# A state-space layer's hand-written round order: cross products to the top, once-a-group work to the middle, exponentials last

## The chip, the cores and the metric

The kernel runs on one core of one Trainium2 chip. A core has engines that each work through their own list of instructions in order: TensorE (PE, matrix products), VectorE (DVE), ScalarE (ACT), GpSimd (POOL) and SyncE (SP, which here only issues DMAs). They wait for each other through semaphores. The metric is device time of one execution in microseconds (us). Three timed runs of the kernel before gave 2692.72, 2696.85 and 2704.56 us, a median of 2696.85.

## The reference, cut to what matters

A decoder of four blocks with twelve layers works on x, 32 sequences of 128 tokens of 128 features. Only the first layer, a state-space layer, is touched:

```
x = x + attn0(layernorm(x))          # then eleven more layers
# attn0, for every sequence, in two chunks of 64 tokens:
z, xBC, dt = split(u @ in_proj.T)            # 256, 512, 32 columns
xBC = silu(causal depthwise conv, 4 taps)    # 256 of x, 128 of B, 128 of C
dt  = 0.001 + 0.099 * sigmoid(dt + dt_bias);  dA = -exp(A_log) * dt
Acum = cumsum(dA in the chunk)
Yd = sum_s (C.B)[q,s] * exp(Acum[q] - Acum[s]) * x[s] * dt[s]       # s <= q, 32 heads of 8
Yo = C . (state of the chunk before) * exp(Acum)                     # chunk 2 only
y  = (Yd + Yo + D*x) * silu(z);  y = y * rsqrt(mean(y^2)) * norm_w
x  = x + layernorm(u) + layernorm(y @ out_proj.T)                    # u: the normalized x
```

## The kernel before, in words

`layer0` treats the 32 sequences in eight groups (`i`) of four (`j`). There is one round per sequence, n = 4i + j, and two rounds of run-up (n = -2 and -1). The order on PE, DVE and ACT is written out by hand: `follow(T, A, V)` makes every instruction of such an engine come after the one recorded before it, so program order is queue order. POOL keeps its written order only in the prologue. All operations are recorded in one helper, so the profile gives nearly all of them line 194; they are told apart by their tiles.

What a round does, with the names used below:

- `first(n+2)`: PE forms decays and C.B for the sequence two rounds on; ACT copies them into a tile `cbl` and takes one exponential; POOL forms `right`. Then PE transposes the convolved x, ACT copies it (the "xt copy", 128x256) and POOL makes two scaled copies `xd`, `xe` and masks `cbl`.
- `second(n+1)`: four matmuls into two `two` tiles (the exponents). `exponentials(n+1)`: two ACT exponentials of 128x1024. `weighted(n+1, h)`: two DVE products of 128x1024 (`bbig<-bbig,cbl`), here called w0 and w1.
- `third(n)`: 64 small products into `acc`, and then the **cross part**: four matmuls (the state of the first chunk, and the decay), an ACT copy into `cbl` (the "cross copy") and a DVE product of 128x128 (`gmid<-cbl`, the "cross product").
- `conv(g, c)`: one of four channel blocks per round, in five steps: matmul and ACT copy; ACT scale; three DVE updates (`gmid<-bmid,w,gmid`); ACT tanh; a last DVE product (`gmid<-bmid,gmid`). Block 2, which falls in the rounds with j = 1, is done by four matmuls over 512 columns instead (`ps<-xnT,taps`, "the taps", 8 instructions in the trace), an ACT activation, a tanh and the last DVE product.

Once a group: `entry(g)` (layer norm of x: statistics; a scale; four ACT activations "xn"; four transposes and their copy; four more ACT activations "x acts" and a POOL addition), `decays(g)` (dt: matmuls; a DVE addition `dts<-ps,ww`; tanh; six DVE steps; a matmul and an exponential; a product), `gate(g, b)` twice (matmul, ACT copy, ACT tanh; a DVE product into `z`) and `joined(g)` in six steps S1 to S6 (S1: D*x plus the sums; S2: times silu(z); S3: two ACT squares and a POOL addition; S4: the output product of 16 instructions and its copy; S5: the mean-square matmul, statistics, `s<-ps`; S6: scale and addition into x).

PE results go through one-bank PSUM tiles `ps`, of which there are two, used in turn: the result after next can't be written before ACT or DVE has read the one two back. `bmid` has five buffers and `gmid` ten, taken in the same way.

Of the kernel before, what the change touches and what calls it, by code (L numbers as in the profile page):

```python
# [23 lines left out]
G = 8  # L24
J = 4
# [180 lines left out]
def program(ctx, tc, cols, x, ctxt, mask, drop, dfirst, dsmall, dwide, drows, dunits, dexperts, dconst, drel, dwq, out):  # L206
    nc = tc.nc
    V, A, T = (Ordered(tc, engine) for engine in (nc.vector, nc.scalar, nc.tensor))
    P, SY = Ordered(tc, nc.gpsimd), nc.sync
# [10 lines left out]
    def ps(shape=(128, 512), dtype=F32):  # L220
        return pp.tile(list(shape), dtype, tag="ps", name="ps", bufs=2)
# [14 lines left out]
    def gmid(shape=(128, 512), dtype=F32):  # L236
        return mid.tile(list(shape), dtype, tag="gmid", name="gmid", bufs=10)
# [42 lines left out]
    ident = K["ident"]  # L280
# [3 lines left out]
    for i in range(G):  # L284
        t = const.tile([128, J, D], F32, name=f"x{i}")
        SY.dma_start(out=t, in_=x[i * J : i * J + J].rearrange("b s d -> s b d"))
        xg.append(t)
        if i == 0:
            SY.dma_start(out=ident, in_=dconst[:, 0:128])
            SY.dma_start(out=cs[:, 128:], in_=dconst[:, 128 : cconst.kept])  # L290
            w0 = units.tile([128, cfirst.n], F32, tag="unit", name="w0")
            A.dma_start(out=w0, in_=dfirst)
            ww = const.tile([128, cwide.n], F32, name="ww")
            A.dma_start(out=ww[:, 0 : cwide.early], in_=dwide[:, 0 : cwide.early].to_broadcast([128, cwide.early]))
    taps = units.tile([128, UNIT], F32, tag="unit", name="taps")
    SY.dma_start(out=ww[:, cwide.early :], in_=dwide[:, cwide.early :].to_broadcast([128, cwide.n - cwide.early]))
    wr = const.tile([1, crows.n], F32, name="wr")
# [17 lines left out]
    onesb = const.tile([128, 128], BF16, name="onesb")  # L315
    V.memset(onesb, 1.0)
    identb = const.tile([128, 128], BF16, name="identb")
    V.tensor_copy(identb, ident)

    pick16 = const.tile([128, 4], BF16, name="pick16")  # L320
    V.tensor_copy(pick16, K["pick16"])
    flip = const.tile([128, 128], BF16, name="flip")
    V.tensor_copy(flip, W0["flip"])
    ctxT = [const.tile([128, 512], F32, name=f"ctxT{i}") for i in range(G)]


# [489 lines left out]
    def layer0(lead):  # L816
# [3 lines left out]
        def weights():  # L820

            A.activation(na, WW["m_A_log"], AF.Exp)
            V.tensor_scalar(na, na, -1.0, None, ALU.mult)
            yield
            for b in range(2):
                mean, block = small(1), W0["out"][:, b * 128 : b * 128 + 128]
                V.tensor_scalar(block, block, W0["norm_w"][:, b : b + 1], None, ALU.mult)
                V.tensor_reduce(mean, block, AX.X, ALU.add)
                V.tensor_scalar(mean, mean, -1.0 / 128, None, ALU.mult)
                V.tensor_scalar(block, block, mean[:, 0:1], None, ALU.add)  # L830
            V.tensor_scalar(W0["D"], W0["D"], 0.25, None, ALU.mult)
            yield

        block2 = W0["xbc"][:, 256:384]
# [2 lines left out]
        def make_taps():  # L837

            d, p = bmid((128, 4, 128)), ps((128, 4, 128))
            V.tensor_tensor(d, bc(ident, 1, 4), bc(W0["cw"][:, 8:12], 2, 128), ALU.mult)  # L840
            mm(flat(p), block2, flat(d))
            A.copy(taps[:, 0:512], flat(p))

        kept = [gbig((128, 2, 1024)) for _ in range(3)]
        more = bbig()
        sides = [kept[0][:, n].rearrange("p (j s r c) -> p j s r c", j=J, s=2, r=4) for n in range(2)]

        def fill():
            for t in (*kept[0:2], more):
                P.memset(t, 0.0)  # L850
            for t in sides:
                for token, side, at in ((0, 0, 0), (64, 0, 8), (0, 1, 16)):
                    one = bc(bc(ident[:, token : token + 1], 1, J), 2, 4)
                    P.tensor_copy(t[:, :, side, :, at : at + 8], one.to_broadcast([128, J, 4, 8]))

        xds = [t.rearrange("p (a n m e) -> p a n m e", a=8, n=4, m=4) for t in (kept[1][:, 0], kept[1][:, 1], more[:, 0:1024])]
        rights = [kept[2][:, n, 0:512].rearrange("p (a k) -> p a k", a=8) for n in range(2)]
# [159 lines left out]
        def third(n):  # L1017

            i, j = n // J, n % J
            (xd, xe, cbl, _), m = fronts.pop(n), mids.pop(n)[0].rearrange("p s h q -> p (s h) q")  # L1020
            if j == 0:
                sums[i] = [acc((128, 2, J, 64)) for _ in range(2)]
                offs[i] = gmid((128, 2, J, 64))
            for b in range(2):
                for k in range(4):
                    for r in range(4):
                        for ch in range(2):
                            rows = slice(64 * ch, 64 * ch + 64)
                            mm(sums[i][ch][32 * r : 32 * r + 32, b, j], flat(xd[rows, 4 * b + r, k]), m[rows, 16 * b + 4 * r + k],
                               k == 0, k == 3)  # L1030
            p = ps((128, 2, 2, 64))
            for b in range(2):
                mm(p[:, 0, b], xe[:, 128 * b : 128 * b + 128], cbl[0:64, 64:128])
            for b in range(2):
                mm(p[:, 1, b], K["spread"][:, 128 * b : 128 * b + 128], cbl[:, 320:384])
            A.copy(cbl[:, 128:384], p.rearrange("p s b q -> p (s b q)"))
            both = cbl[:, 128:384].rearrange("p (s b q) -> p s b q", s=2, b=2)
            V.tensor_tensor(offs[i][:, :, j], both[:, 0], both[:, 1], ALU.mult)
# [50 lines left out]
        def go(what, g, *more):  # L1089

            if 0 <= g < G:
                key = what, g, *more
                if key not in late:
                    late[key] = what(g, *more)
                next(late[key], None)
# [6 lines left out]
        go(entry, 0)  # L1102
        go(entry, 0)
        fill()
        make_taps()
        go(entry, 0)
        next(prepared)
        go(conv, 0, 2)
        go(decays, 0)
        go(conv, 0, 3)  # L1110
        go(conv, 0, 2)
        go(entry, 1)
        go(conv, 0, 3)
        go(decays, 0)
        go(conv, 0, 2)
        go(conv, 0, 3)
        go(conv, 0, 0)
        go(decays, 0)
        go(entry, 1)
        go(conv, 0, 3)  # L1120
        go(conv, 0, 0)
        go(conv, 0, 1)
        go(decays, 0)
        go(conv, 0, 3)
        go(entry, 1)
        go(conv, 0, 0)
        go(conv, 0, 1)
        go(conv, 0, 0)
        go(conv, 0, 1)
        go(entry, 1)  # L1130
        go(conv, 0, 0)
        go(decays, 0)
        go(conv, 0, 1)
        go(conv, 0, 1)
        next(prepared)
# [2 lines left out]
        for n in range(-2, G * J):  # L1138
            i, j = n // J, n % J

            convs_now = [(1, 2)] if n == -2 else [(1, 3), (1, 0)] if n == -1 else [(i + 1, 1) if j == 0 else (i + 2, (2, 3, 0)[j - 1])]

            def go_conv():
                for g, c in convs_now:
                    go(conv, g, c)

            front = first(n + 2) if n + 2 < G * J else iter(())
            next(front, None)
            go_conv()
            next(front, None)  # L1150
            go_conv()
            if j == 0:
                go(decays, i + 1)
                go(gate, i, 0)
                go(joined, i - 2)
            elif j == 1:
                go(joined, i - 1)
            elif j == 2:
                go(decays, i + 2)
                go(decays, i + 2)  # L1160
                go(entry, i + 3)
                go(joined, i - 1)
            elif j == 3:
                go(gate, i + 1, 1)
                go(entry, i + 3)
                go(joined, i - 1)
            if 0 <= n + 1 < G * J:
                second(n + 1)
            go_conv()
            if 0 <= n + 1 < G * J:  # L1170
                exponentials(n + 1)
            if j == 1:
                go(joined, i - 1)
            elif j == 3:
                go(entry, i + 3)
            if 0 <= n + 1 < G * J:
                weighted(n + 1, 0)
            if 0 <= n < G * J:
                third(n)
            if 0 <= n + 1 < G * J:  # L1180
                weighted(n + 1, 1)
            if j == 0:
                go(entry, i + 2)
                go_conv()
            elif j == 1:
                go(entry, i + 2)
            elif j == 2:
                go(decays, i + 2)
                go(gate, i + 1, 1)
                go_conv()  # L1190
            elif j == 3:
                go(joined, i)
                go(gate, i + 1, 0)
                go_conv()
                go(decays, i + 2)
            go_conv()
            if n == -1:
                go(entry, 1)
            if n >= G * J - 5:
                next(lead)  # L1200
        next(lead)
        go(joined, G - 1)
# [1311 lines left out]
```

## Time and profile before

| | us |
|---|---|
| median of three timed runs (range) | 2696.85 (2692.72 to 2704.56) |
| the profiled execution's own time | 2692.69 |
| its span in the trace | 2690.9 |
| the first layer in it, roughly | 0 to 327 |
| busy in 90 to 270 us (180 us): PE, DVE, ACT, POOL | 166.6, 160.8, 122.4, 94.5 |

A timeline line reads: start in us, time taken, engine, line, operation, tile written <- tiles read, shape, number of merged instructions, and in brackets the engine's idle time before it with what ended it. `PE` is the matmul, `PEld` the load of its weights. A line of the windows view gives the stretch, its length, the busy time of each engine asked for with the count of instructions, then the TensorE clock that was granted (1.00 is full), the DMA share and GB/s.

### The profile page before, as it was taken

The page shows a single profiled execution, that of the slowest core. Times are in us where ns is not written, and L with a number is a line of the kernel's source. Part 1 is how long each engine was busy: PE and PEld are TensorE (multiplying, and loading weights), DVE is VectorE, ACT ScalarE, POOL GpSimd, SP SyncE. Part 2 cuts the span into 40 slices and gives each one's busy share as a digit, 9 for nine tenths or more (in the row PEclk, how much of TensorE's full clock was granted, in tenths as well). Part 3 has the DMA queues.
Part 4 walks back from the last instruction along what each step waited for, and adds up shares of the span by engine and source line. Part 5 has one row for each costly group of instructions (what it writes and reads, how often), then busy time and mean ns, then how long its engine had stood idle before and what let it go on. Part 6 is the DMA issues. An engine that isn't in the chain of part 4 may idle for free.

```text
span 2690.9 us, 59184 instructions
## 1 busy us (share of the span) xinstructions
PE 2387.5 (89%) x24663; PEld 1527.2 (57%) x24663; DVE 1983.8 (74%) x3972; ACT 1347.3 (50%) x2999; POOL 927.1 (34%) x979
## 2 busy tenths in 40 slices
PE   6999889999989999999998999988888987887755
PEld 3665567777744435556764444446665886544434
DVE  6888778888888756777776555569996338898993
ACT  5766544444422223344443445468983334665653
POOL 3454532322310214345651101144443444332432
PEclk8999899999999999999998999999998998998886
DMA  3000000000000010000000000000003463100000
GB/s 113 3 2 14 10 21 5 9 5 4 18 12 1 0 36 3 3 14 14 12 3 17 1 0 1 1 1 2 2 2 129 147 214 130 62 16 16 28 12 20
DMA packets 51966, 74.23 MB, mean 28 GB/s; under 512 B 4017, under 2 KB 42450, under 8 KB 51570
## 3 DMA queue, kind: packets, MB, share of 16 engines
q1 hardware_dynamic: 48786, 64.10, 7.5%
q0 software_dynamic: 2624, 5.40, 0.6%
q8 instruction: 194, 3.18, 0.5%
q10 hardware_dynamic: 288, 0.95, 0.1%
q14 instruction: 74, 0.61, 0.1%
HBM read 57.54 MB, written 12.89 MB: 26 GB/s over the span
## 4 chain that ended last, share of the span: by engine, by line
PE 56%; DVE 22%; ACT 6%; issue 2%; POOL 2%; DMA 0%; DVEq 0%; ACTq 0%; POOLq 0%
PE two L194 20%; PE ps L194 18%; PE acc L194 17%; DVE bbig L194 9%; DVE s L194 7%; ACT bbig L194 3%; DVE bmid L194 3%; POOL xn L194 1%; DVE x L194 1%; ACT bmid L194 1%; DVE gmid L194 1%; POOL s L194 1%; DVE h L194 0%; ACT L194 0%; ACT gmid L194 0%
## 5 line engine op out<-in xcount | busy, mean ns | idle before, releaser
L194 PE MATMUL two<-xnT,u 128*128 128x512 f32 x512 | 261.7, 612 | 9.3 <-ACT bmid L194 5.6
L194 DVE TENSOR_REDUCE s<-two 128x8 f32<-128x1024 f32 (+1 forms) x192 | 228.8, 1219 | 47.6 <-PE two L194 43.0
L194 DVE TENSOR_TENSOR bbig<-bbig 128x1024 f32<-128x1024 f32 (+3 forms) x232 | 248.2, 1111 | 14.3 <-ACT bbig L194 12.0
L194 PE MATMUL acc<-bmid,u 128*128 128x512 f32 x416 | 215.0, 603 | 13.4 <-DVE bmid L194 12.4
L194 PE MATMUL ps<-cs,bbig 128*128 128x128 f32 x1184 | 176.5, 289 | 47.6 <-ACT bbig L194 21.3
L194 DVE TENSOR_TENSOR bmid<-bmid,ps 128x512 f32<-128x512 f32 x192 | 129.9, 684 | 93.1 <-ACT bmid L194 71.0
L194 PEld LDWEIGHTS ps<-cs,bbig 128*128 128x128 f32 x1184 | 135.1, 146 | 101.2 <-ACT bbig L194 36.5
L194 PE MATMUL two<-gbig,gmid 32*128 32x512 f32 (+1 forms) x1248 | 186.3, 551 | 4.4 <-issue 2.1
L194 POOL TENSOR_TENSOR s<-s,nhalf 128x4 f32<-128x4 f32 x104 | 128.7, 1237 | 135.1 <-DVE s L194 116.5
L194 PEld LDWEIGHTS two<-xnT,u 128*128 128x128 f32 x512 | 91.4, 191 | 115.7 <-issue 56.6
L194 ACT ACTIVATE bbig<-two 128x1024 f32<-128x1024 f32 x96 | 94.8, 1025 | 116.7 <-PE acc L194 101.7
L194 DVE RECIPROCAL s<-acc 128x128 f32<-128x128 f32 x96 | 91.3, 951 | 83.6 <-PE acc L194 83.4
L194 ACT COPY bbig<-ps 128x512 f32<-128x512 f32 x166 | 91.4, 585 | 116.4 <-PE ps L194 116.3
L194 POOL TENSOR_TENSOR x<-x,ww 128x512 f32<-128x512 f32 x64 | 91.6, 1431 | 163.1 <-ACT xn L194 80.3
L194 ACT ACTIVATE bmid<-two,ws 128x512 f32<-128x512 f32 x128 | 85.2, 686 | 111.6 <-PE two L194 111.4
L194 POOL TENSOR_TENSOR bbig<-bbig,s 128x1024 f32<-128x1024 f32 x32 | 61.7, 1927 | 222.6 <-PE two L194 152.5
L194 ACT ACTIVATE bmid<-two 128x512 f32<-128x512 f32 x88 | 52.5, 597 | 164.0 <-PE two L194 159.2
L194 PEld LDWEIGHTS acc<-bmid,u 128*128 128x128 f32 x416 | 75.0, 192 | 101.0 <-issue 46.1
L194 ACT ACTIVATE bbig<-two,s 128x256 f32<-128x256 f32 x256 | 118.1, 477 | 25.4 <-DVE s L194 25.3
L194 ACT ACTIVATE bbig<-bbig,s 128x128 f32<-128x128 f32 x384 | 118.8, 390 | 6.8 <-DVE s L194 6.8
L194 POOL TENSOR_SCALAR gbig<-bmid,cs 128x512 f32<-128x512 f32 x64 | 99.2, 1566 | 49.0 <-ACT bmid L194 49.0
L194 PE MATMUL two<-xT,we 128*128 128x128 f32 (+1 forms) x576 | 100.4, 330 | 15.9 <-ACT xT L194 9.8
(331 smaller groups left out, 6267.0 us busy)
## 6 DMA issues: line engine op xcount, KB each, us to landing
we<-in_experts SPq DMA_DIRECT2D x36, 768.0 KB, 4.6
u<-in_units SPq DMA_DIRECT2D x10, 768.0 KB, 4.3
gmid<-in_ctx SPq DMA_DIRECT2D x16, 256.0 KB, 3.0
x<-in_x SPq DMA_DIRECT2D x8, 256.0 KB, 5.6
gmid<-in_mask SPq DMA_DIRECT2D x8, 256.0 KB, 3.1
ys<-bbig SPq DMA_DIRECT2D x2, 1024.0 KB, 6.2
gmid<-ys SPq DMA_DIRECT2D x8, 256.0 KB, 3.1
gmid<-in_drop SPq DMA_DIRECT2D x8, 256.0 KB, 3.5
```

Source lines behind the costliest of these rows:

```text
L194: d = self.made = f(*args, **kwargs)
```

## The change

The cross part becomes a function of its own, `cross(n)`, called at the very top of round n, ahead of `first(n+2)`; `third(n)` keeps the 64 small products. The once-a-group steps that stood between the exponentials and w0, and many of those that stood after w1, go to the middle of a round, ahead of `second(n+1)`; what is left after w1 is the end of the convolution and few steps. S3 and S4 now stand together in the round with j = 2. The prologue is put in another order (block 3's convolution and the first `decays` ahead of the taps), the first two DMAs on ACT's queue change places, three small DVE casts move from the program's start into the weights' preparation, one of `fill`'s three memsets is taken first, and the next layer's first preparatory step is taken one round earlier.

```diff
-            A.dma_start(out=w0, in_=dfirst)
             ww = const.tile([128, cwide.n], F32, name="ww")
             A.dma_start(out=ww[:, 0 : cwide.early], in_=dwide[:, 0 : cwide.early].to_broadcast([128, cwide.early]))
+            A.dma_start(out=w0, in_=dfirst)
...
-    V.tensor_copy(identb, ident)
...
-    V.tensor_copy(pick16, K["pick16"])
...
-    V.tensor_copy(flip, W0["flip"])
...
             V.tensor_scalar(W0["D"], W0["D"], 0.25, None, ALU.mult)
+            V.tensor_copy(identb, ident)
+            V.tensor_copy(pick16, K["pick16"])
+            V.tensor_copy(flip, W0["flip"])
             yield
...
+        def cross(n):
+            i, j = n // J, n % J
+            _, xe, cbl, _ = fronts[n]
+            if j == 0:
+                offs[i] = gmid((128, 2, J, 64))
             p = ps((128, 2, 2, 64))
             for b in range(2):
                 mm(p[:, 0, b], xe[:, 128 * b : 128 * b + 128], cbl[0:64, 64:128])
...
-        go(entry, 0)
+        go(conv, 0, 3)
+        go(decays, 0)
+        go(conv, 0, 3)
+        go(conv, 0, 2)
...
+            if 0 <= n:
+                cross(n)
             front = first(n + 2) if n + 2 < G * J else iter(())
...
                 go(joined, i - 2)
+                go(entry, i + 2)
             elif j == 1:
                 go(joined, i - 1)
+                go(entry, i + 2)
             elif j == 2:
                 go(decays, i + 2)
+                go(joined, i - 1)
+                go(joined, i - 1)
                 go(decays, i + 2)
+                go(gate, i + 1, 1)
                 go(entry, i + 3)
-                go(joined, i - 1)
             elif j == 3:
                 go(gate, i + 1, 1)
+                go(gate, i + 1, 0)
+                go(decays, i + 2)
                 go(entry, i + 3)
                 go(joined, i - 1)
             if 0 <= n + 1 < G * J:
...
                 exponentials(n + 1)
-            if j == 1:
-                go(joined, i - 1)
-            elif j == 3:
-                go(entry, i + 3)
-            if 0 <= n + 1 < G * J:
                 weighted(n + 1, 0)
...
             if j == 0:
-                go(entry, i + 2)
                 go_conv()
-            elif j == 1:
-                go(entry, i + 2)
             elif j == 2:
                 go(decays, i + 2)
-                go(gate, i + 1, 1)
+                go(entry, i + 3)
                 go_conv()
             elif j == 3:
                 go(joined, i)
-                go(gate, i + 1, 0)
                 go_conv()
-                go(decays, i + 2)
             go_conv()
...
-            if n >= G * J - 5:
+            if n >= G * J - 6 and n != G * J - 5:
                 next(lead)
```

More of the change, by code (lines that the diff above doesn't have):

```diff
@@ L848, in fill @@
         def fill():
-            for t in (*kept[0:2], more):
-                P.memset(t, 0.0)
+            P.memset(kept[0], 0.0)
             for t in sides:
@@ L854, in fill @@
                     P.tensor_copy(t[:, :, side, :, at : at + 8], one.to_broadcast([128, J, 4, 8]))
+            for t in (kept[1], more):
+                P.memset(t, 0.0)
         xds = [t.rearrange("p (a n m e) -> p a n m e", a=8, n=4, m=4) for t in (kept[1][:, 0], kept[1][:, 1], more[:, 0:1024])]
@@ L1019, in third @@
             i, j = n // J, n % J
-            (xd, xe, cbl, _), m = fronts.pop(n), mids.pop(n)[0].rearrange("p s h q -> p (s h) q")
+            xd, m = fronts.pop(n)[0], mids.pop(n)[0].rearrange("p s h q -> p (s h) q")
             if j == 0:
                 sums[i] = [acc((128, 2, J, 64)) for _ in range(2)]
-                offs[i] = gmid((128, 2, J, 64))
             for b in range(2):
@@ L1104, in layer0 @@
         fill()
+        go(entry, 0)
         make_taps()
-        go(entry, 0)
+        go(conv, 0, 3)
+        go(decays, 0)
+        go(conv, 0, 3)
+        go(conv, 0, 2)
+        go(decays, 0)
+        go(entry, 1)
+        go(conv, 0, 3)
         next(prepared)
+        go(decays, 0)
+        go(conv, 0, 0)
         go(conv, 0, 2)
@@ L1110, in layer0 @@
         go(conv, 0, 3)
+        go(conv, 0, 0)
         go(conv, 0, 2)
@@ L1113, in layer0 @@
         go(conv, 0, 3)
-        go(decays, 0)
-        go(conv, 0, 2)
-        go(conv, 0, 3)
+        go(conv, 0, 1)
+        go(conv, 0, 0)
+        go(entry, 1)
+        go(conv, 0, 1)
         go(conv, 0, 0)
@@ L1119, in layer0 @@
         go(entry, 1)
[L1120 to L1126, printed above, removed]
         go(conv, 0, 1)
         go(conv, 0, 0)
[L1129 to L1132, printed above, removed]
         go(conv, 0, 1)
```

## The prediction

> **What bounds the kernel now.** The change touches only the first layer, so I read the stretch it takes. First the windows view over 90 to 270 us, a steady part of that layer (VectorE's busy time stands third, behind the two columns of PE):
>
> ```profile
> 90.00:270.00 180.00, 166.60 (x3172) 109.74 (x3174) 160.77 (x305) 122.35 (x248) 94.50 (x94) 0.94 0.02 7
> ```
>
> PE (166.6 of 180) and DVE (160.8) are both nearly full, so neither alone sets the pace: what matters is where one waits for the other. The waits view of that stretch, DVE only:
>
> ```profile
> DVE gmid L194 <- ACT bmid L194: 6.2, 3, 2.6
> DVE dts L194 <- PE ps L194: 6.2, 5, 1.3
> DVE gmid L194 <- ACT cbl L194: 3.8, 7, 0.9
> DVE bbig L194 <- ACT bbig L194: 0.9, 3, 0.3
> ```
>
> 17 us of waits: for the tanh of block 2 (6.2), for the matmuls of `decays` (6.2), for the cross copy (3.8; this one the change attacks), for exponentials (0.9). Then the timeline of the group where they are shortest, from the end of DVE's three updates with j = 0 (call it X, 136.6) to the addition `dts` with j = 2 (call it Y, 148.0):
>
> ```profile
> 136.03 3.66 PE L194 MATMUL ps<-xnT,taps 128*128 128x512 f32 x8
> 136.55 1.21 DVE L194 SCALAR_TENSOR_TENSOR bbig<-bbig,cbl 128x1024 f32<-128x1024 f32 x1
> 139.73 0.69 ACT L194 ACTIVATE gmid<-ps,w 128x512 f32<-128x512 f32 x1 [1.94 <-PE ps L194]
> 140.57 0.64 ACT L194 ACTIVATE bmid<-gmid 128x512 f32<-128x512 f32 x1
> 141.10 1.94 ACT L194 ACTIVATE bbig<-two 128x1024 f32<-128x1024 f32 x2
> 142.91 1.17 ACT L194 ACTIVATE bmid<-z 128x512 f32<-128x512 f32 x2
> 143.95 0.39 ACT L194 COPY cbl<-ps 128x256 f32<-128x256 f32 x1
> 144.20 1.67 ACT L194 ACTIVATE x<-x,s 128x128 f32<-128x128 f32 x4
> 146.17 0.61 ACT L194 COPY bmid<-ps 128x512 f32<-128x512 f32 x1
> 146.84 1.08 PE L194 MATMUL ps<-w,xnT 128*128 128x32 f32 x8
> 148.03 0.29 DVE L194 TENSOR_TENSOR dts<-ps,ww 128x128 f32<-128x128 f32 x1 [1.12 <-PE ps L194]
> ```
>
> The chain to Y runs taps, block 2's activation and tanh, exponentials, squares (1.17), cross copy, x acts (1.67), copies, `decays`. The exponentials end at 143.0, before DVE takes w0 at 143.3: hidden. Starts of neighbours lie closer than the durations say (w0 to next 1.14, two exponentials 1.81, x acts 1.55); I use these spacings. X to Y is 11.4, 11.5, 14.7, 13.1 and 14.7 us in the groups from 98.8, 136.6, 173.2, 213.5 and 251.7, and 16.1 in the first (60.9 to 77.0): mean 13.6. Y to the next X is 26.3, 25.2, 25.5, 25.2 and 24.9 (21.8 in the first group, without `joined`). The long X to Y have a reason on PE:
>
> ```profile
> 171.65 1.22 PE L194 MATMUL ps<-w,gbig 128*128 128x64 f32 x4 [1.03 <-ACT cbl L194]
> 173.53 6.10 PE L194 MATMUL ps<-xnT,taps 128*128 128x512 f32 x8
> ...
> 172.00:179.00 7.00, 7.00 (x17) 0.54 0.00 0
> ```
>
> Here the granted clock was 0.54 (last line, windows view, PE only) and the taps took 6.10 us, not 3.66.
>
> **The change, step by step.** All instructions stay; only places move.
>
> 1. *X to Y.* Before, block 2's taps stood behind a `ps` bank that the cross copy and the xnT copy freed ahead of the tanh of block 1, so they began 0.5 us before X. Now ACT does that tanh first (it waits for X: 0.1 + 0.55), then the cross copy (0.4), whose bank the taps take: they start at X + 1.1, end at X + 4.75. Activation and xt copy to 5.6, tanh to 6.25. Then the x acts, now ahead of the exponentials: 7.75; first exponential 8.7, second 9.6; cross copy 9.95. DVE is through w0, w1, block 1's last product, cross product and S2 at X + 4.3 (2.28 + 0.6 + 0.2 + 1.2), waits 2.0 for the tanh, does 0.6, waits 1.8 for the exponential, does w0, w1, cross product (to 11.2). PE's next conv matmul (1.1) needs the cross copy's bank: 11.05; its copy 11.6; `decays` 1.0: Y = X + 12.75. That is 1.3 over the undisturbed 11.45, though the squares (1.05) have left the chain.
>
> 2. *The clock.* In rounds with j = 0 the four transposes of `entry` now stand behind the conv copy, and that waits on ACT for DVE's last product of the round before (before, ACT waited 2.49 us there, but PE had other work). Laid out, PE is through at Y + 17.9 and gets the copy at 21.2: idle 3.3 us, then 5.2 us of work before the taps. In the trace, 1.0 to 1.2 us of idleness at that place was followed by the half clock in three groups of the last four with taps, and not in 134.96. If half clock follows, 6.8 us long as at 172, the 5.2 us become about 8.6, a start of the taps 2.2 later: X + 14.95. With as many such groups as before (4 of 6): (2 x 12.75 + 4 x 14.95) / 6 = 14.2; with all, 14.95. Against 13.6: +0.6 to +1.35, six times: +3.7 to +8.1; without any, 12.75: -5. I take +5.5. The Trainium skill ("TensorE: Matmul & The Clock Gate", "What's actually happening") says the clock falls to half after an idle window of about 3.4 us and comes back after a busy one; the row at 172 agrees in length (two such windows), not in the idleness needed (1.0). By that rule a 3.3 us idle stretch is at the edge in every group: 6 x 1.35 = 8.1, speaking against the change.
>
> 3. *Y to X, j = 2.* `gate`'s matmul (1.1), copy and tanh (1.1) now precede the exponentials: first exponential at Y + 4.95, DVE free at 3.7 to 4.1: +0.85. *j = 3:* the mean-square matmul now queues behind a second `gate`, through two `ps` banks: conv copy Y + 8.95, gate matmul 10.1, its copy 10.75, mean-square 11.85; DVE is there at 10.1 to 10.95 and waits 1.0 to 1.8: 1.4. Ends for both together: nothing, if ACT and PE run further ahead than laid out, and 2.65. The rest of the stretch is DVE alone: 22.9 before, plus one cross product (0.2).
>
> 4. *POOL's part in DVE's time.* Before, 25.2 - 22.9 = 2.3 us of Y to X is lengthening, as in `z<-bmid,z` at 1.53 (157.16, beside a POOL operation) against 0.68 at 167.97. Where a wait follows, it is swallowed. Kept: nothing to 2.2; I take 0.8 to 1.1, as only the stretch after step 3's wait has none behind it. Y to X = 23.1 + 2.25 + 0.95 = 26.3 to 26.8 against 25.2 to 25.5: +1.2 to +1.5, five times, and +0.5 in the first group: +7.5.
>
> 5. *Cross product.* The 3.8 us of waits for its copy are inside the stretches above; now the copy is long done.
>
> 6. *Prologue.* The casts (0.23, 0.17, 0.22) leave the first norm, but its next DVE instructions read constants landing at 9.81, so xn still starts near 10.6. Transposes ahead of the taps' making bring xnT from 15.84 to 13.3; statistics (1.5) and three updates (2.2) fall into DVE's 6.9 us wait before 23.15; but `decays` stays behind block 2's activation on ACT (24). Laying the rest end to end, the second `dts` (42.02) comes at 39.5: -2.5 (ends: 0, if the taps stay cold longer; -5). The weights' DMA, issued 0.43 later, had landed by 9.16 and is needed at 10.6: nothing; if not, up to +0.5. `fill`'s order: nothing, as the first fold waits for DVE.
>
> 7. *End.* In the last rounds the cross product waited 0.63 to 0.71; its chain is gone: -1 (0 to -2). The next layer's step a round earlier: 0 +- 1.
>
> Sum: 5.5 + 7.5 - 2.5 - 1 = +9.5 on the profiled execution's own 2692.69 (span 2690.9): 2702.2. That execution was the fastest of those shown, 4.2 below the median 2696.85; in terms of that median 2706.
>
> **Rivals.**
> - *Slower by more.* PE's idle stretch brings half clock in every group and reaches into the taps: 6.10 for 3.66, so Y = X + 12.75 + 2.4 + 0.9 (other matmuls): +2.5 x 6 = 15; and DVE's lengthening stays at 2.2: +2.5 x 5 = 12.5. With -2.5: +25, 2722. For it: PE's share of 0.93; against: taps start after most of the half-clock stretch. It decides when PE's stop lasts over a second longer than the 1.0 to 1.2 that sufficed.
> - *Faster.* PE keeps its full clock: with conv and cross at the top, the 1.0 to 1.2 us stop right ahead of the taps is gone, and nothing halves the clock: X to Y 12.75 for 13.6, -0.85 x 6 = -5; Y to X at 24.4 (waits of step 3 hidden, half the lengthening), -0.8 x 5 = -4; -3.5 for prologue and end: -12.5, between -8 and -22 (the lower end if none of the 17 us of waits comes back): 2684. For it: two groups (98.8, 136.6) show it can stay full; against: step 2's idle stretch. It decides where no window of PEclk in a j = 0 to 1 stretch falls under 0.9.
>
> **Numbers.** My case 0.50 (+3 to +17; a fifth of it beyond +13.5), slower by more 0.28, faster 0.22. A measurement of this kernel tells about 0.5%, 13.5 us, from no change. Slower: 0.28 + 0.10 = 0.38. Faster: a little over half of the faster case lies beyond -13.5 us if it is as wide as its bounds: 0.12. Same: 0.50. My case alone: 2700 to 2714; to hold eight in ten the range takes in most of both rivals: 2682 to 2724.
>
> **What would show it.** DVE waits of 1.5 to 2 us in every group for block 2's tanh (`gmid<-bmid` from ACT) and then for w0 (`bbig` from ACT); about 1 us for `s<-ps` from PE; no waits for `gmid<-cbl`; PEclk near 0.5 around each j = 0 to 1 turn; the second `dts` near 39.5; Y to Y near 40 us for 37.8 to 39.9. I am wrong if w0 with j = 1 starts less than 7 us after X, or if the layer's last DVE product falls before 327.

## The result and the profile after

| | before | after |
|---|---|---|
| median of eight runs each on one chip, us (range) | 2694.78 (2686.91 to 2704.56) | 2707.28 (2701.53 to 2711.34) |
| ratio after / before | | 1.0044, 95% interval 1.0022 to 1.0065 |
| span of the profiled execution, us | 2690.9 | 2705.3 |

The changed kernel is slower by 0.44%, 12.5 us; +9.5 us was predicted, put as 2706 against the earlier median of 2696.85. The traces show the stop on PE that the prediction named, but also that three terms of the sum were mis-sized. Their errors cancelled, so how close the total came is luck.

The windows view of the changed kernel over 90 to 270 us (columns as for before):

```profile
90.00:270.00 180.00, 156.76 (x2865) 103.76 (x2866) 146.75 (x291) 111.57 (x221) 78.81 (x84) 0.87 0.01 2
```

Every engine does less in the same 180 us, DVE 146.8 us for 160.8, and the granted clock is 0.87 for 0.94. The waits view says for what DVE waits (90 to 275 us):

```profile
DVE gmid L194 <- ACT bmid L194: 22.0, 4, 7.1
DVE bbig L194 <- ACT bbig L194: 7.2, 4, 1.8
DVE dts L194 <- PE ps L194: 2.0, 4, 0.5
```

and for what PE waits:

```profile
PE ps L194 <- ACT bmid L194: 18.2, 13, 3.5
PE ps L194 <- ACT cbl L194: 3.1, 5, 1.7
```

DVE no longer waits for the cross copy. It waits 7 us for block 2's tanh in three of these four groups (1.0 in the other), and PE stops for 3.3 to 3.5 us ahead of `entry`'s transposes in four of groups 2 to 6. The timeline of one turn from j = 0 to j = 1 shows how the two hang together:

```profile
172.18 0.38 PE L194 MATMUL ps<-cs,gmid 128*128 128x128 f32 x2
175.44 0.58 ACT L194 COPY bmid<-ps 128x512 f32<-128x512 f32 x1 [3.67 <-DVE gmid L194]
176.08 1.12 PE L194 MATMUL ps<-cs,xn 128*128 128x128 f32 x4 [3.51 <-ACT bmid L194]
180.94 2.35 DVE L194 SCALAR_TENSOR_TENSOR bbig<-bbig,cbl 128x1024 f32<-128x1024 f32 x2
181.12 0.63 ACT L194 ACTIVATE bmid<-gmid 128x512 f32<-128x512 f32 x1
183.38 0.37 ACT L194 COPY cbl<-ps 128x256 f32<-128x256 f32 x1 [1.63 <-PE ps L194]
184.91 5.45 PE L194 MATMUL ps<-xnT,taps 128*128 128x512 f32 x7
192.32 0.69 DVE L194 SCALAR_TENSOR_TENSOR gmid<-bmid,gmid 128x512 f32<-128x512 f32 x1 [7.02 <-ACT bmid L194]
194.83 2.56 DVE L194 SCALAR_TENSOR_TENSOR bbig<-bbig,cbl 128x1024 f32<-128x1024 f32 x2 [1.81 <-ACT bbig L194]
198.94 0.29 DVE L194 TENSOR_TENSOR dts<-ps,ww 128x128 f32<-128x128 f32 x1 [0.51 <-PE ps L194]
```

ACT's conv copy waits 3.67 us for a `bmid` buffer that DVE's last product of the round before frees; PE's transposes of `entry` wait for the bank behind that copy; then X (180.94), and Y comes 18.0 us later. The windows view, PE only, of the same turn (length, busy, granted clock):

```profile
172.00:176.00 4.00, 0.56 (x3) 0.97 0.01 4
176.00:189.00 13.00, 12.92 (x163) 0.50 0.01 1
190.00:200.00 10.00, 9.18 (x182) 1.00 0.01 2
```

After the stop PE runs 13 us at half clock, which takes in the taps (5.45 us for seven of their eight instructions in the line above, 5.87 for all eight).

Where the 14.4 us between the two spans come from, read off at X and Y of each group in both traces, and at one marker behind the first layer, the next layer's first product `bbig<-bbig,s` (367.29 us before, 379.28 after):

| stretch | before | after | difference |
|---|---|---|---|
| start to the first X | 60.9 | 57.5 | -3.4 |
| X to Y, six groups | 16.1, 11.4, 11.5, 14.7, 13.1, 14.7 | 18.6, 12.95, 17.9, 18.0, 18.0, 18.1 | +22.0 |
| Y to X, six times | 21.8, 26.3, 25.2, 25.5, 25.2, 24.9 | 21.5, 26.3, 26.3, 26.3, 26.3, 26.3 | +4.0 |
| last X to the marker | 75.9 | 65.4 | -10.5 |
| marker to the end | 2323.6 | 2326.0 | +2.4 |

The last row is the same program in both; in the traces shown in this document it takes between 2320 and 2333 us, and eight runs of before alone spread over 18 us, so it is taken as scatter here.

### The profile page after: what moved, and what is told of

Read it like the earlier page. It is cut to its first block, busy times and chain, and to the rows that moved or that the text cites. A ratio compares the mean times of both kernels' runs of the same rounds, so it can differ in the third digit from the quotient of the medians.

```text
span 2705.3 us, 59213 instructions
## 1 busy us (share of the span) xinstructions
PE 2391.3 (88%) x24644; PEld 1532.2 (57%) x24663; DVE 1983.4 (73%) x3972; ACT 1347.6 (50%) x2999; POOL 920.2 (34%) x979
## 4 chain that ended last, share of the span: by engine, by line
PE 62%; DVE 24%; ACT 8%; issue 3%; POOL 2%; DMA 1%; SPq 0%; DVEq 0%; ACTq 0%; POOLq 0%
PE ps L194 24%; PE two L194 21%; PE acc L194 18%; DVE bbig L194 9%; DVE s L194 7%; ACT bbig L194 4%; DVE bmid L194 3%; DVE gmid L194 2%; ACT bmid L194 1%; POOL xn L194 1%; DVE x L194 1%; POOL s L194 1%; DMA we<-in_experts 1%; ACT gmid L194 0%; ACT xn L194 0%
## 5 line engine op out<-in xcount | busy, mean ns | idle before, releaser
L194 DVE TENSOR_REDUCE s<-two 128x8 f32<-128x1024 f32 (+1 forms) x192 | 228.8, 1219 | 48.9 <-PE two L194 44.2
L194 PE MATMUL ps<-cs,bbig 128*128 128x128 f32 x1184 | 177.5, 290 | 46.5 <-ACT bbig L194 21.1
L194 PEld LDWEIGHTS two<-xnT,u 128*128 128x128 f32 x512 | 91.4, 191 | 115.6 <-issue 56.6
L194 PE MATMUL two<-xT,we 128*128 128x128 f32 (+1 forms) x576 | 102.2, 334 | 13.7 <-ACT xT L194 9.8
```

The lines of the kernel that those rows point to most:

```text
L194: d = self.made = f(*args, **kwargs)
```

## The experiments

Theory: PE's 3.5 us stop at `entry`'s transposes brings the half clock, and that makes X to Y long. Rivals: the chain alone does it (the taps' bank behind block 1's tanh, x acts ahead of the exponentials), whatever the clock; or half clock comes anyway from shorter stops. In the table, "layer" is the time of the marker above in the run's trace less 367.29, from one execution each (it can lie at the edge of the run's range, as in e3).

| run | median, us | ratio to before (95%) | X to Y, groups 2 to 6 | layer |
|---|---|---|---|---|
| before | 2694.8 | | 11.4, 11.5, 14.7, 13.1, 14.7 | 0 |
| after | 2707.3 | 1.0044 (1.0022 to 1.0065) | 12.95, 17.9, 18.0, 18.0, 18.1 | +12.0 |
| e1 entry back | 2695.1 | 1.0003 (0.9990 to 1.0016) | 12.9, 14.8, 14.7, 14.9, 14.6 | -1.5 |
| e2 warm | 2694.1 | 1.0004 (0.9989 to 1.0020) | 13.1, 12.95, 14.7, 14.9, 14.6 | -4.8 |
| e3 entry alone | 2703.3 | 1.0036 (1.0019 to 1.0053) | 11.7, 13.5, 13.3, 16.9, 14.0 | +0.9 |
| e4 lead back | 2713.8 | 1.0072 (1.0051 to 1.0094) | 12.95, 17.9, 18.0, 18.05, 18.1 | +15.6 |
| e5 entry back, late tanh | 2686.4 | 0.9983 (0.9967 to 0.9999) | 11.5, 11.9, 12.9, 13.7, 14.2 | -10.3 |
| e6 bmid six | 2692.4 | 1.0003 (0.9990 to 1.0017) | 12.9, 14.65, 14.6, 14.6, 15.0 | -7.7 |
| e7 bmid six, late tanh | 2675.9 | 0.9947 (0.9925 to 0.9969) | 12.5, 10.7, 10.7, 10.7, 13.05 | -13.5 |
| e8 prologue alone | 2689.9 | 0.9998 (0.9981 to 1.0015) | 11.4, 13.0, 11.5, 13.1, 14.7 | -7.8 |
| e9 cross alone | 2723.2 | 1.0115 (1.0089 to 1.0142) | 14.0, 14.0, 14.1, 18.6, 16.4 | +17.9 |
| e10 e7 + PE mean square | 2688.7 | 0.9991 (0.9973 to 1.0008) | 12.6, 11.3, 10.8, 10.8, 12.5 | -13.0 |
| e11 late tanh alone | 2707.7 | 1.0049 (1.0029 to 1.0070) | 12.5, 18.1, 18.1, 18.1, 18.1 | +13.5 |
| e12 e7 + first group | 2680.6 | 0.9945 (0.9926 to 0.9963) | 11.25, 10.7, 10.7, 10.4, 10.7 | -19.0 |

Each set of four had its own runs of before beside it, with medians of 2694.9 (e1 to e4), 2691.3 (e5 to e8) and 2695.0 (e9 to e12); the ratios are what to compare.

### e1: the transposes back behind w1

```diff
             if j == 0: ...
                 go(joined, i - 2)
-                go(entry, i + 2)
...
             if j == 0:
+                go(entry, i + 2)
                 go_conv()
```

> After, with only the four transposes of entry and their copy (rounds with j = 0) put back behind w1. Theory 'PE's stop': the 3.5 us for which PE waits there behind the conv copy (ps from bmid) brings the half clock that then doubles the taps; without it the taps take 3.66 us in every group, X to Y is 12.9 as in the one undisturbed group of the changed kernel, not 18.0, so five groups give back 5.0 each: 2707.3 - 25 = about 2682. Rival 'the chain': X to Y grew because the taps' bank waits for block 1's tanh and the x acts stand ahead of the exponentials, whatever the clock: taps may change, X to Y stays 17 to 18, 2704 to 2711. Rival 'half clock anyway': shorter stops of 1.0 to 1.2 us, as before the change, halve it in about four groups of six: 2694 to 2700.

Measured: 1.0003; X to Y 14.6 to 14.9 in four groups. Moving one step back undoes the slowdown, so the place of `entry`'s transposes carries it. (The gains at the start and the end are still in e1; without them it would be slower than before, as its X to Y is.) But the clock did not hold: the taps took 5.3 to 5.5 us. PE's timeline in e1:

```profile
168.54 0.66 PE L194 MATMUL ps<-cs,xn 128*128 128x128 f32 x4 [0.48 <-ACT bmid L194]
171.83 1.22 PE L194 MATMUL ps<-w,gbig 128*128 128x64 f32 x4 [1.46 <-ACT xnT L194]
174.52 5.45 PE L194 MATMUL ps<-xnT,taps 128*128 128x512 f32 x8 [0.74 <-ACT cbl L194]
```

The 3.5 us stop is gone, and three shorter ones (0.48, 1.46, 0.74) stand in the same stretch. So theory and third rival are each half right: removing the long stop is worth 3.3 us a group, not 5, because a shorter half clock follows the short stops in these four groups (not in the first of the five, where the taps took 3.66 us behind a stop of 1.70).

### e2: useless matmuls in the stop

```diff
                 go(joined, i - 2)
+                if 0 <= n and i + 2 < G:
+                    early[n + 1] = [two((128, 2, 8, 64)) for _ in range(2)]
+                    for r in range(3):
+                        mm(early[n + 1][0][:, r % 2]..., ident, cs[:, 0:512])
                 go(entry, i + 2)
...
-            segs = [two((128, 2, 8, 64)) for _ in range(2)]
+            segs = early.pop(n, None) or [two((128, 2, 8, 64)) for _ in range(2)]
```

> After, with three useless matmuls of 128x512 added on PE ahead of entry's transposes in the rounds with j = 0 (at the taps' 3.66 us for four, 2.75 us of work at full clock), into a tile that second takes over right after. Nothing else moves. Theory 'PE's stop': they fill the 3.5 us stop, the clock stays at 1.0, the taps take 3.66 us and X to Y falls from 18.0 to 13 or 14: 2683 to 2690, faster although PE has more to do. Rival 'the chain': nothing gained, 2707 to 2712, taps at 5.8.

Measured: 1.0004, an interval that doesn't meet that of after (1.0022 to 1.0065). PE's timeline in e2:

```profile
165.77 2.74 PE L194 MATMUL two<-cs 128*128 128x512 f32 x6
169.23 0.66 PE L194 MATMUL ps<-cs,xn 128*128 128x128 f32 x4 [0.72 <-ACT bmid L194]
175.22 5.36 PE L194 MATMUL ps<-xnT,taps 128*128 128x512 f32 x8 [0.74 <-ACT cbl L194]
```

This is the cleanest test of the clock: no instruction is moved, PE gets 2.7 us more work in each of six rounds, and the ratio falls by 0.4%, 11 us. The chain alone as a cause is out. Where the useless work ran (165.8 to 168.5) PE reached the taps at full clock; but the 0.74 us stop right ahead of them (1.02 in one group) was followed by half clock in the last three groups, and at 135.99, after the same stop, it was not (3.66 us).

### e3: the transposes alone, in the kernel before

```diff
                 go(joined, i - 2)
+                go(entry, i + 2)
...
             if j == 0:
-                go(entry, i + 2)
                 go_conv()
```

> Before, with only entry's transposes in the rounds with j = 0 moved into the middle, ahead of second, as the change has them. Theory 'PE's stop': the stop of 3 us and more appears, half clock in every group, the taps at 5 to 6 us, X to Y from a mean of 13.6 to 16 to 18: +12 to +25, 2707 to 2720. Rival 'the chain': the place of the transposes alone does nothing, 2692 to 2698.

Measured: 1.0036, 8 us, less than the least expected. In the profiled execution the stop is shorter and the clock mostly holds:

```profile
169.11 0.66 PE L194 MATMUL ps<-cs,xn 128*128 128x128 f32 x4 [2.34 <-ACT bmid L194]
175.07 3.66 PE L194 MATMUL ps<-xnT,taps 128*128 128x512 f32 x8
```

The same 2.34 us stop at 207.60 was followed by half clock (taps 5.67 us, X to Y 16.9). So the move alone costs, but less than in the changed order, where the stop is 3.5 us. The profiled execution (2696.1) was the fastest of e3's nine, so where the median's 8 us went is not seen in this trace.

### e4: the next layer's step one round later again

```diff
-            if n >= G * J - 6 and n != G * J - 5:
+            if n >= G * J - 5:
```

> After, with only the condition of the next layer's preparatory steps put back (first step taken one round later, as before). The two traces show the changed kernel 21 us behind at Y of the sixth group and 12 us behind when the first layer's last statistics are done: some 10 us come back in its last rounds. Theory 'lead': the preparatory step taken earlier brings them, so without it 2714 to 2719. Rival 'order': the cross part at the top and the exponentials last bring them, 2706 to 2709.

Measured: 2713.8 and 1.0072 against 1.0044; the intervals overlap. In the traces the last X to the marker takes 68.8 us for 65.4. So the earlier step brings 3.4 us of the 10.5 in the trace (6.5 in the medians). What it removes can be seen at the end of the kernel before: the step's transposes stood in PE's way while POOL made their input, and w0 waited.

```profile
325.74 0.48 PE L194 MATMUL ps<-cs,xn 128*128 128x128 f32 x1 [3.57 <-POOL xn L194]
328.15 0.48 PE L194 MATMUL ps<-cs,xn 128*128 128x128 f32 x1 [1.94 <-POOL xn L194]
335.57 1.23 DVE L194 SCALAR_TENSOR_TENSOR bbig<-bbig,cbl 128x1024 f32<-128x1024 f32 x1 [7.97 <-ACT bbig L194]
```

In the changed kernel the four of them run in one piece:

```profile
346.78 0.60 PE L194 MATMUL ps<-cs,xn 128*128 128x128 f32 x4
```

The other 7 us of the end's gain were not isolated; with the cross part alone at the top (e9) the end takes 74.3 us, so alone it brings 1.6 of them; what it brings in the changed order was not measured.

### e5 to e7: the two stops, singly and together

`bmid six` gives the conv copy a sixth buffer (a `cbl` buffer pays for the room):

```diff
-CBLS = 4
+CBLS = 3
...
-... tag="bmid", name="bmid", bufs=5)
+... tag="bmid", name="bmid", bufs=6)
```

`late tanh` takes block 1's tanh and last product from the end of the round with j = 0 to behind the next round's cross copy:

```diff
             next(front, None)
+            if j == 1 and n > 0:
+                go(conv, i + 1, 1)
             go_conv()
+            if j == 1 and n > 0:
+                go(conv, i + 1, 1)
...
-            if j == 0:
-                go_conv()
-            elif j == 2:
+            if j == 2:
...
-            go_conv()
+            if j != 0:
+                go_conv()
```

e5 is e1 with the late tanh, e6 is after with six buffers, e7 is after with both.

> As e1_entry_back (entry's transposes behind w1), and block 1's tanh and last product moved from the end of the round with j = 0 to the next round's top, behind the cross copy and first's copies on ACT. In e1_entry_back (2695.1) PE still stopped 0.74 us right ahead of the taps for the bank that the cross copy frees, because ACT did that tanh first, which waits for X; the taps took 5.3 to 5.5 us and X to Y was 14.6 to 14.9. Theory 'stops before the taps': with that stop gone the clock holds, the taps take 3.66 us, X to Y is 11.5 to 12.9, four groups give back 2 to 3 each: 2683 to 2688. Rival 'the other stop': the 1.5 us for which PE waits for the xnT copy in the same stretch is enough by itself for the half clock: 2692 to 2698, taps above 5.

> After, order untouched, with six bmid buffers for five (and three cbl for four, to make room). The conv copy in the rounds with j = 0 then has a buffer without waiting for DVE's last product of the round before. Theory 'PE's stop by the buffer': the 3.5 us stop goes, ACT no longer waits 3.67 us there, X to Y falls from 18.0 to between 12.9 and 14.8 (the 0.74 us stop ahead of the taps is left): 2685 to 2696. Rival 'the chain': X to Y stays 17 to 18, 2704 to 2710.

> After with six bmid buffers (three cbl), and block 1's tanh and product behind the next round's cross copy, as in e5_entry_back_late_tanh; entry's transposes stay in the middle. Theory: neither the 3.5 us nor the 0.74 us stop is left, the granted clock is 1.0 through every j = 0 to 1 turn, the taps take 3.66 us, X to Y is 11.5 to 12.9: five groups by 5 to 6.5 us under the changed kernel's 18.0: 2675 to 2684, faster than both kernels. Rival 'half clock anyway': some other stop of 0.5 to 1 us halves it in most groups: 2688 to 2698.

Measured: e5 0.9983, e6 1.0003, e7 0.9947. In e6 PE's stop at the transposes is 0.46 us, and PE, now far ahead, stops later for the bank of the taps:

```profile
164.08 0.66 PE L194 MATMUL ps<-cs,xn 128*128 128x128 f32 x4 [0.46 <-ACT bmid L194]
173.02 5.36 PE L194 MATMUL ps<-xnT,taps 128*128 128x512 f32 x8 [3.69 <-ACT cbl L194]
```

They start at X + 1.1, as the prediction laid them out, but in half clock: 14.65 us for 12.75. With the late tanh as well (e7, timeline of PE, DVE and ACT) nothing stands ahead of the taps:

```profile
165.26 0.66 PE L194 MATMUL ps<-cs,xn 128*128 128x128 f32 x4 [0.46 <-ACT bmid L194]
170.44 3.66 PE L194 MATMUL ps<-xnT,taps 128*128 128x512 f32 x8
173.46 2.35 DVE L194 SCALAR_TENSOR_TENSOR bbig<-bbig,cbl 128x1024 f32<-128x1024 f32 x2
173.64 0.63 ACT L194 ACTIVATE bmid<-gmid 128x512 f32<-128x512 f32 x1 [2.52 <-DVE gmid L194]
180.30 3.32 DVE L194 SCALAR_TENSOR_TENSOR bbig<-bbig,cbl 128x1024 f32<-128x1024 f32 x2
184.17 0.28 DVE L194 TENSOR_TENSOR dts<-ps,ww 128x128 f32<-128x128 f32 x1
```

The taps begin 3.0 us ahead of X instead of 4.0 behind it, no DVE line in this stretch has a wait, and X to Y is 10.7 us: DVE's own work. In 90 to 270 us DVE is busy 170.7 us (146.8 in after). The expected full clock in every turn came in three of groups 2 to 6: half clock from 89.8 to 93.2 and from 233.2 to 246.8 us went ahead of the two others, and X to Y there is 12.5 and 13.05. e7 beats both kernels, by 0.5% and 1.0% (0.9947 / 1.0044 = 0.990). In e5 the taps were at 3.66 us in three of the five groups listed and above 4.9 in two; stops of 1.5 us for the xnT copy were left in two turns.

### e8: the prologue alone

Before, with the diff's part ahead of the rounds and nothing else.

> Before, with only the change's prologue: the two DMAs of ACT's queue, the three casts, fill's memset and the written order ahead of the rounds; the rounds and the end are those of before. The prediction took -2.5 for this; in the changed kernel's trace the second dts came 5.0 earlier and the end of the first three updates 3.4 earlier than before. If that is the prologue's: 2690 to 2692.5. If the rounds of before take it back in their own waits: 2693 to 2697.

Measured: 2689.9 against 2691.3, ratio 0.9998: no difference that the runs can tell from none, and compatible with the 2.5 us expected. In the trace the second `dts` came at 37.72 for 42.02 and the first X at 56.6 for 60.9: -4.3 there.

### e9: the cross part alone at the top

```diff
+        def cross(n): ...          # the last lines of third, unchanged
...
+            if 0 <= n:
+                cross(n)
             front = first(n + 2) if n + 2 < G * J else iter(())
```

> Before, with only the cross part taken out of third and called at the top of the next round. What it was moved for, 3.8 us of DVE's waits for the cross copy in 90 to 270 us, is gone in any case. Theory 'bank': the taps' bank now comes free only behind block 1's tanh and the cross copy, PE stops 0.7 us and more right ahead of the taps as in e1_entry_back, the taps take over 5 us in most groups and X to Y is 14 to 15 for the mean of 13.6: 2695 to 2702. Rival 'wait gone': X to Y at 11.5 to 12.8 and the 3.8 us show as a gain: 2684 to 2690.

Measured: 1.0115, 28 us, far outside both expectations, and the waits for the cross copy are not gone (5.0 us in 90 to 270). The reason is not the one expected either; ACT, PE and DVE in the round with j = 2:

```profile
145.54 1.17 ACT L194 ACTIVATE bmid<-z 128x512 f32<-128x512 f32 x2
146.58 1.65 ACT L194 ACTIVATE x<-x,s 128x128 f32<-128x128 f32 x4
148.12 0.70 ACT L194 COPY cbl<-ps 128x256 f32<-128x256 f32 x2
148.54 1.12 PE L194 MATMUL ps<-xnT,w 128*128 128x512 f32 x2 [1.40 <-ACT cbl L194]
151.54 0.29 DVE L194 TENSOR_TENSOR dts<-ps,ww 128x128 f32<-128x128 f32 x1 [1.78 <-PE ps L194]
```

At the top of the next round the cross copy stands behind squares and x acts, which the old order puts at the end of a round; the next conv matmul needs its bank, `decays` the one after. X to Y is 14.0 even where the taps run at full clock (3.66 us). In the changed order, where squares and x acts stand elsewhere, those waits are gone; so it seems that the once-a-group moves to the middle make the cross part bearable at the top, and that the change's parts can't be priced one by one and added. The moves without the cross part were not run.

### e10: POOL's addition taken over by PE

```diff
-            P.tensor_tensor(sq[0], sq[0], sq[1], ALU.add)
...
-                mm(msp[:, j : j + 1], sq[0][:, j], K["ones"][:, 0:1])
+                for b in range(2):
+                    mm(msp[:, j : j + 1], sq[b][:, j], K["ones"][:, 0:1], b == 0, b == 1)
```

> e7_bmid_six_late_tanh (2675.9), with POOL's addition of the two squares left out and the mean-square matmul summing both squares in PSUM instead (four more small matmuls a group). With j = 2 the three updates after Y take 3.40 us beside POOL's power and that addition, 2.74 in before beside the power alone, 2.29 beside nothing. Theory 'POOL lengthens DVE': they fall to about 2.75, Y to X from 26.4 to 25.7, six groups: 2671 to 2673. Rival 'not POOL': they stay at 3.4, or PE's extra time (half of the 1.02 us for eight) is paid: 2675 to 2680.

Measured: 2688.7, 0.9991 for e7's 0.9947: slower, and outside both expectations, although the theory's first half came true. The updates after Y, in e7 beside POOL's addition:

```profile
148.46 3.41 DVE L194 SCALAR_TENSOR_TENSOR gmid<-bmid,w,gmid 128x508 f32<-128x508 f32 x3
150.05 1.28 POOL L194 TENSOR_TENSOR bmid<-bmid 128x512 f32<-128x512 f32 x1
```

and in e10 without it:

```profile
145.68 2.30 DVE L194 SCALAR_TENSOR_TENSOR gmid<-bmid,w,gmid 128x508 f32<-128x508 f32 x3
148.69 2.36 DVE L194 SCALAR_TENSOR_TENSOR bbig<-bbig,cbl 128x1024 f32<-128x1024 f32 x2 [0.71 <-ACT bbig L194]
156.57 0.16 DVE L194 TENSOR_SCALAR s<-ps 128x4 f32<-128x4 f32 x1 [0.83 <-PE ps L194]
```

The whole 1.1 us was this addition (four groups of five show it; POOL's power still ran beside the updates). But the moment it is gone, the wait for w0's exponential (0.71) appears that step 3 of the prediction had laid out (0.85), and the mean-square wait with it (0.83, here behind a doubled matmul). Y to X grew to 26.7 to 28.2 us from 26.2 to 26.9, 4.9 us over the six. The layer as a whole is only 0.5 us later in the trace than in e7, because e10's first group, left out of the table, happened to be 4.6 us shorter (13.9 for 18.5; the last section shows the same between e6 and e7). The rest of the ratio's difference, some 12 us in all, is not explained.

### e11: the late tanh alone

The second of the two edits of e7 on the changed kernel, five buffers.

> After, with only block 1's tanh and product moved behind the next round's cross copy; five bmid buffers and entry's transposes as the change has them. It completes the square with the changed kernel (18.0 us from X to Y), e6_bmid_six (14.65) and e7_bmid_six_late_tanh (10.7). Theory 'the 3.5 us stop is the larger cause': it stays, the half clock still reaches through the taps, X to Y is 16 to 17.5: 2699 to 2706. Rival 'the tanh's place is the larger cause': X to Y 11 to 14, 2678 to 2692.

Measured: 1.0049, X to Y 18.1, no gain at all. The waits of PE and of DVE in 90 to 270 us:

```profile
PE ps L194 <- ACT bmid L194: 18.0, 13, 3.5
```

```profile
DVE gmid L194 <- ACT bmid L194: 18.2, 7, 3.9
```

With the square complete (18.0; late tanh 18.1; six buffers 14.65; both 10.7): the sixth buffer is worth 3.4 us a group by itself, the late tanh nothing by itself and another 3.9 once the buffer is in. The long stop hides what the short one costs.

### e12: the first group

```diff
+            late_convs = [(1, 3), (1, 0)] if n == 0 else [(i + 1, 1)] if j == 1 and n > 0 else []
...
-            if n == -1:
+            if n == 0:
                 go(entry, 1)
```

and the run-up's last tanhs and products are taken at `late_convs` in round 0.

> e7_bmid_six_late_tanh (2675.9), with the x acts of group 1 moved from the run-up's end to the end of round 0, and the run-up's last tanhs and products behind round 0's cross copy. In e7 the first group has PE stopped for 4.51 us at 45.5 us, half clock from there, taps at 5.79 and X to Y 18.5 where the later groups have 10.7. Theory 'stops bring half clock': with the stop cut to 3 us or less the first group's X to Y falls to 11 to 14: 2668 to 2672. Rival: the run-up is bound by something else, no gain: 2674 to 2678.

Measured: 0.9945, the same as e7. The first group's X to Y stayed at 18.0: PE's stop there fell from 4.51 to 1.92 us and the half clock came all the same, so the theory missed:

```profile
48.52 2.07 PE L194 MATMUL ps<-xnT,w 128*128 128x512 f32 x2 [1.92 <-ACT cbl L194]
```

The later groups are all at 10.4 to 11.3, and DVE's waits in 90 to 275 us are down to one line:

```profile
DVE bbig L194 <- ACT bbig L194: 0.3, 1, 0.3
```

In this stretch the layer is now bound by DVE (busy 177.5 of the 180 us from 90 to 270). The layer ended 5.5 us earlier than in e7's trace; the medians don't show that gain.

## Why the prediction was right, and where it was not

The time and its sign were right, and so was the source of the slowdown: step 2's stop of 3.3 us was 3.5, for the reason given (`ps` bank, conv copy, `bmid`, DVE's last product), and e1, e2 and e6 show that this stop carries the slowdown. How far the half clock behind it reaches was wrong in the central case, and only other errors brought the total back: that part is luck. Term by term:

1. *X to Y laid out:* 12.75 predicted, 12.95 in the one group at full clock, where the taps began 1.1 us after X, as laid out. Waits there: 1.0 for the tanh (2.0 laid out), 1.8 for w0 (1.8), 0.5 for `dts` (1.5). Right in sum.
2. *The clock:* mis-sized, +3.7 us a group measured for +0.9. The prediction let the half clock last 6.8 us, as at 172 us before, and so end at the taps; it lasted 13.7 and took the taps in. That is the place of the rival "slower by more", which priced it at Y = X + 16.05; 18.0 was measured. Its condition, a stop "over a second longer" (a slip: 1 us was meant), was met: 3.5 against 1.0 to 1.2 (1.32 in the last group, which step 2 read as 1.2). In before, 1 us stops had been followed by half clock only sometimes; here all four groups with the long stop had it. The first group's 18.6 is another case: its half clock followed a 4.50 us stop of the run-up (e12).
3. *Waits in Y to X:* 2.25 taken, none seen. The chosen value was the wrong end of "nothing, and 2.65". e10, one edit away from e7, shows why for w0: its wait was covered by the lengthening that step 4 priced beside it. The two overlap and were added. For the mean-square wait no run shows it cleanly.
4. *POOL's lengthening:* 0.8 to 1.1 taken; DVE's busy time in Y to X rose from 24.64 to 25.81, a cross product of 0.2 among it: about right. Steps 3 and 4 together: +7.5 predicted, +4.0 measured.
5. *Cross product:* its waits went, as said; in e9 they did not, so this was probably owed to the squares and x acts moving away, which step 5 didn't say.
6. *Prologue:* -2.5 predicted, -3.4 at the first X; the second `dts` came at 37.0, not 39.5. The lower end (-5) was the one for `dts`.
7. *End:* -1 predicted, -10.5 measured, the largest miss after step 2. Only the cross chain was counted; the next layer's step was put at 0 +- 1, but its transposes had been in the way in the last rounds (e4: 3.4 of it in the trace).

The sum held by luck: step 2 was 16.5 us too low (22.0 for 5.5), and steps 3 and 4, 6 and 7 together 13.9 too high (3.5, 0.9 and 9.5). What I had set as signs: the tanh wait (7 us instead of 2), the w0 wait and the missing `gmid<-cbl` waits appeared, the `s<-ps` wait did not, and Y to Y was 44.2, not 40.

## What to carry to other kernels

Before moving an instruction on TensorE, follow the PSUM bank that it will be queued for back to the engine that frees it, and further to the buffer which that engine waits for; if the answer is an engine that is behind, the move makes a stop, and half clock can follow it: in these traces between none (behind 1.65 us in after) and 17.1 us of it (behind 1.92 us in e12). One more buffer for the tile at the root of that chain, and a wait taken out of the path of the bank's copy, turned a 0.4% loss into a 0.5% gain with every moved step left in its new place. A wait and lengthened instructions ahead of it on the same engine overlap, as in e10: price them as the larger of the two, not as their sum. Test pairs of stops together, since removing one of two may show nothing.

## What the runs showed of the hardware

The half clock came in pieces of about 3.4 us: in every trace of this case its stretches in the first 330 us last 3.4, 6.8, 10.2, 13.7 or 17.1 us. From 1 us windows, taking the mean clock of the first and last one as a mixture of 1.0 and 0.5, for example: 173.46 to 176.88 in e6 (3.4), 171.34 to 178.16 in e1 (6.8), 175.72 to 189.38 in after (13.7). A stop of 0.74 us was followed by one such piece (175.68 to 179.08) in e2 and by none at 136.0, though a stop of 0.7 or 0.9 us stood 6 us ahead of both. The length doesn't follow from the stop's length: 3.7 us of it ahead of the taps cost 3.4 us of half clock in e6, 3.5 us ahead of smaller matmuls cost 13.7 in after. Nor does it follow from what runs behind the stop. In the first group PE has the same 4.51 us stop and the same matmuls behind it in e6 and in e7 (timeline, then windows, PE only); e6:

```profile
50.59 2.08 PE L194 MATMUL ps<-xnT,w 128*128 128x512 f32 x2 [4.51 <-ACT cbl L194]
...
54.00:61.00 7.00, 7.00 (x162) 1.00 0.01 2
```

and e7:

```profile
50.04 2.08 PE L194 MATMUL ps<-xnT,w 128*128 128x512 f32 x2 [4.51 <-ACT cbl L194]
...
54.00:61.00 7.00, 7.00 (x150) 0.50 0.01 2
```

In e6 the half clock lasted 6.8 us and X to Y was 13.9, in e7 17.1 us and 18.5 (e10, in e7's order, has 6.8 us and 13.9 too). What differs in the traces is when the half clock began: 1.1 us into the stop in e6 (47.2), 3.3 us into it in e7 (48.9). So a part of the differences in X to Y above can be chance of this kind. Where half clock came turn after turn, Y to Y also settled near whole numbers of pieces: 44.2 to 44.4 us in after and in e11 (13 pieces of 3.41 are 44.4), 40.9 to 41.1 in e1 (12 are 41.0); a small saving inside such a turn may show nothing for that reason, which was not tried. What decides the length was not tried, and stays open.

The Trainium skill ("TensorE: Matmul & The Clock Gate", "What's actually happening") describes a free-running window of about 3.4 us, which agrees with the pieces measured, and a clock that drops after an idle window and returns after a busy one. The return disagrees: in the changed kernel PE was busy 12.92 of the 13 us from 176 to 189, as the profile counts it, and the clock stayed at 0.50 throughout. The drop in the changed kernel agrees, behind a stop of 3.51 us; in e2 it disagrees, where the half clock at 175.68 followed stops of 0.72 and 0.74 us. And a 1.65 us stop in after was followed by none:

```profile
98.65 3.66 PE L194 MATMUL ps<-xnT,taps 128*128 128x512 f32 x8 [1.65 <-ACT cbl L194]
```

A POOL addition of 1.28 us lengthened DVE's updates by 1.1 us, nearly its own length (e7 against e10). The Trainium skill ("SBUF — State Buffer", "SBUF: two separate sides") says that a DVE operation with two inputs in SBUF and a POOL operation that reads SBUF take turns at a shared port for a whole instruction; these two numbers agree with that.
